# A bidirectional WKV network on one core: products, means and gelu of neighbouring steps put in another order

## The chip, the cores and the metric

The kernel runs on one core of a Trainium2 chip. The metric is the time of the program on the device in microseconds (us), the median of several runs. The engines are PE (TensorE: matmuls), DVE (VectorE), ACT (ScalarE), POOL (GpSimd) and SP, which here only issues DMAs. Each engine works through its own instructions in the order in which the program issues them, and semaphores make it wait for the others.

## The reference

x has shape (16, 192, 56, 56). Three layers of one kind are followed by a fourth of another, and each adds its result to x:

```python
x = x + _L0_conv_ref(_gn(x), ...)   # and L1, L2: the same with other weights
x = x + _L3_conv_ref(_gn(x), conv_w, ...)
```

`_gn` normalises groups of 6 channels over the image. One of the first three layers computes, for the T = 3136 positions of an image:

```python
k, v, r = xs @ Wk.T, xs @ Wv.T, xs @ Wr.T
x_fwd = wkv_scan(real_w, u, k, v)                    # a decaying sum along T, numerator over denominator
x_bwd = flip(wkv_scan(real_w, u, flip(k), flip(v)))  # the same from the end
h = sigmoid(r) * 0.5 * (x_fwd + x_bwd)
h = layernorm(h)                                     # over channels
out = h @ Wo.T
```

The fourth layer takes the largest difference to the four pixels two rows or columns away, puts it beside x, multiplies 384 channels by a 192 x 384 matrix, and applies a normalisation with constants and gelu.

## The kernel before, in words

**Tiling.** Images are taken in eight pairs. With 192 channels a pair has 384, which lie in three column blocks j of 128 partitions; a tile is 128 x 3 x 448 floats, and a pair has NL = 7 such chunks (L = 448 positions). A `Run` is one pair in one layer.

**Two passes.** A WKV layer goes over the chunks forwards (units "A") and then backwards (units "B"). Unit A forms k (`a_keys`), exp k (`a_exp`), v (`a_values`), their product (`a_ekv`, L940), the two scans on DVE (`a_q`, `a_p`, L875), denominator and numerator with the bonus (`a_den`, `a_num`, L890), inverts the denominator by ln and exp on ACT (`invert`, L975 and L978) and multiplies on POOL (`a_y`, L982). Unit B scans backwards (`b_q`, `b_p`), adds the bonus (`b_den`, `b_num`), inverts, forms r on PE (`b_gate`: `product`, L597 to L607) and the sigmoid of r on ACT in two halves (`b_exp`, L996, an exp that reads r; `b_sigmoid`, L1003 and L978), and mixes on POOL (`b_mix`, nine operations, L1031 to L1033). Then comes layernorm: squares on ACT (`b_squares`, L1040), sums over channels on PE (`b_sums`, L1047 and L1049), the square of the mean on ACT (`b_rs1`, L1055), its subtraction by a matmul (`b_rs2`, L1059), ln and exp on ACT (`b_rs3`, L1063 and L1065), the spread over partitions on PE (`b_spread`, L1071), the scaling on DVE (`b_scale`, L1076), the output product (`b_out`), the addition to x (`b_x`, L1089, called by `add`), and the new chunk's statistics on ACT (`b_stats`, by `sum_up`).

**The conv layer** has units "C": `c_rows` and `c_columns` on DVE (L1108 to L1129), two products accumulated in the same PSUM banks (`c_product` with half 0 and 1), `c_gelu` on ACT (L1150, with a table load before it and one after it, L1155), `c_add` on POOL (L1159) and the store by SP.

**Order.** Two streams of pairs are interleaved: while one run goes backwards, a run of the other goes forwards. The list `steps` holds 249 steps (numbered from 0 here), each with a B unit, a front unit (A or C), or one of them. `with tc.manual_schedule(...)` has each engine's instructions in the order in which the step functions issue them, so the order is written out by hand:

- `both_a_first` (L1379) and `both_a` (L1323): a B and an A unit. There are 17 groups of one first step and five `both_a`, which begin at steps 8, 16, 24, 32, 40, 78, 86, 94, 102, 140, 148, 156, 164, 202, 210, 218 and 226. In the nine groups of 24, 32, 40, 86, 94, 102, 148, 156 and 164, the five `both_a` steps also compute statistics of a pair still to come (`count`, `z_stats`, L734 and L735); the other eight hold none or next to none.
- `both_c` (L1426): a B and a C unit; seven groups of six, at 48, 63, 110, 125, 172, 187 and 234. In all but the last group, the fifth step starts the next pair (`begin_later`) and the sixth has the first A unit of that pair behind it (`ahead`).
- `forward_a`, `forward_c`, `backward_alone` (L1667) and `neither`: steps with one unit or none.

What is late is carried over: a B unit's layernorm begins in its own step and ends in the next (`late[u]` holds its stage). `nback` and `nfront` are the next step's units. In `both_a` the next unit's r is formed at the head of a step (`b_gate(*nback[1:])`, L1330), read by `b_exp` at once, and the layernorm's sums stand last on PE in the step (L1367).

The normalisation ahead of a layer is folded into its weights in four parts (`norm_sums`, `norm_var`, `norm_fold`, `norm_fold_r`), which `gap()` takes one at a time from the list `norms` wherever a step calls it. When conv products are still outstanding (`convs`), the next run is put into `waiting` and its weights are loaded behind the last of these products (`conv_part`). `store()` writes out the chunk that `c_add` has put into `stores` before.

Of the kernel before, what the change touches and what calls it, by code (L numbers as in the profile page):

```python
# [55 lines left out]
NL = T // L  # L56
# [417 lines left out]
def fast_path(ctx: ExitStack, tc: tile.TileContext, flag, x, wproj, wfold, wcfold, wconst, wgroup, sums, picks, vecs, out):  # L474
# [345 lines left out]
        load_ahead(("C" if run.l == NLAYERS else "A", run, 0))  # L820

    def gap(eng=V):
        if norms:
            part, run = norms.pop(0)
            if part is norm_fold:
                part(run, eng)
            else:
                part(run)
# [155 lines left out]


    def b_gate(run, c):
        product(run, "r", run.w[2], run.xb[c], c == NL - 1)

    def b_exp(run, c):
        if c == NL - 1:  # L990
# [166 lines left out]
    def c_add(run, c):  # L1157
        xs, g = run.xa.pop(c), run.ml.pop(c)
        G.tensor_add(g.t, g.t, xs.t)  # L1159
        xs.give()  # L1160
        if c == NL - 1:
            require_all(run.chk, slice(3 * NL + 9, NCHK))
        stores.append((run, c, g))

    def c_end(run, c, more):
# [154 lines left out]
        for _ in range(min(most, len(z))):  # L1320
            z_stats(*z.pop(0))

    def both_a(b, a, nback, nfront, z, loads):  # L1323

        den = lambda: a[0].den[a[1]]
        l = of_stage(0.5)
        load_ahead(nback)
        store()
        if nback is not None:
            b_gate(*nback[1:])  # L1330
            b_exp(*nback[1:])
        count(z)
        b_q(*b)
        if l:
            b_rs2(*l)
            b_rs3(*l)
        b_sigmoid(*b)
        a_values(*a)
        if l:
            b_spread(*l)  # L1340
        b_p(*b)
        b_den(*b)
        for js in (AC, slice(1, 2)):
# [12 lines left out]
        keys(nfront)  # L1356
        a_q(*a)
        if l:
            add(l)
        b_squares(*b, (0,))  # L1360
        a_save(*a)
        count(z)
        exp_keys(nfront, (0, 2))
        b_squares(*b, (2,))
        exp_keys(nfront, (1,))
        b_squares(*b, (1,))
        b_sums(*b)  # L1367
        a_p(*a)
        gap()
        a_den(*a)  # L1370
        b_rs1(*b)
        late[b] = 0.5
        invert(den())
        gap()
        a_num(*a)
        a_y(*a)
        gap()

    def both_a_first(b, a, nback, nfront, loads):  # L1379

        den = lambda: a[0].den[a[1]]
        l = of_stage(0)
        load_ahead(nback)
        store()
        a_values(*a)
        b_squares(*l, (0, 2))
        b_q(*b)
        b_sigmoid(*b)
        b_p(*b)
        b_den(*b)  # L1390
        invert(b[0].ek[b[1]])
        b_num(*b)
        b_mix(*b)
        for u in loads:
            load_ahead(u)
        a_ekv(*a)
        b_squares(*l, (1,))
        if nback is not None:
            b_gate(*nback[1:])
        b_sums(*l)  # L1400
        b_rs1(*l)
        if nback is not None:
            b_exp(*nback[1:])
        a_q(*a)
        b_rs2(*l)
        b_rs3(*l)
        keys(nfront)
        a_p(*a)
        spread_and_scale(l)
        b_squares(*b, (0,))  # L1410
        a_save(*a)
        exp_keys(nfront)
        b_squares(*b, (2, 1))
        b_sums(*b)
        a_den(*a)
        b_rs1(*b)
        late[b] = 0.5
        invert(den())
        a_num(*a)
        add(l)  # L1420
        a_y(*a)
# [4 lines left out]
    def both_c(b, a, nback, nfront, loads):  # L1426

        l0, l1 = of_stage(0), of_stage(1.5)
        load_ahead(nback)
        first = nback is not None and not l1  # L1430
        store()
        b_q(*b)
        b_p(*b)
        if l1:
            b_out(*l1)
        if first:

            b_gate(*nback[1:])
            b_exp(*nback[1:])
            c_product(*a, 0)  # L1440
        if half:
            c_product(*half[0], 1)
        if l0:
            b_squares(*l0, (0,))
        sum_up()
        if l0:
            b_squares(*l0, (2, 1))
            b_sums(*l0)
        if l1:
            add(l1)  # L1450
        b_den(*b)
        invert(b[0].ek[b[1]])
        if l0:
            b_rs1(*l0)
            b_rs2(*l0)
            b_rs3(*l0)
        gap()
        if half:
            u = half.pop()
            c_gelu(*u, False)  # L1460
            c_add(*u)
        for u in loads:
            load_ahead(u)
        if nback is None:
            keys(nfront)
            exp_keys(nfront)
        elif not first:
            b_gate(*nback[1:])
            b_exp(*nback[1:])
        if l0:  # L1470
            b_spread(*l0)
        if not first:
            c_product(*a, 0)
        c_rows(*a)
        gap()
        c_columns(*a)
        gap()
        b_num(*b)
        b_sigmoid(*b)
        b_mix(*b)  # L1480
        if nback is not None:
            if l0:
                b_scale(*l0)
                late[l0] = 1.5
            b_q(*nback[1:])
            b_p(*nback[1:])
            half.append(a)
        else:
            ahead = nfront is not None and nfront[0] == "A"
            if ahead:  # L1490
                a_q(*nfront[1:])
                a_save(*nfront[1:])
            c_product(*a, 1)
            c_end(*a, False)
            if ahead:
                a_values(*nfront[1:])
            if l0:
                b_scale(*l0)
                b_out(*l0)
                late[l0] = 2  # L1500
        late[b] = 0
# [165 lines left out]
    def backward_alone(b, nback, nfront):  # L1667
        load_ahead(nback)
        load_ahead(nfront)
        store()  # L1670
        sum_up()
        b_q(*b)
        gap()
        b_den(*b)
        gap()
        invert(b[0].ek[b[1]])
        b_sigmoid(*b)
        b_p(*b)
        gap(G)
        b_num(*b)  # L1680
        b_mix(*b)
        for u in list(late):
            finish(u)
        if nback is not None:
            b_gate(*nback[1:])
            b_exp(*nback[1:])
        keys(nfront)
        exp_keys(nfront)
        late[b] = 0
# [13 lines left out]
    with tc.manual_schedule(engines={PE.engine, V.engine, S.engine, G.engine, nc.sync.engine}):  # L1703
# [6 lines left out]
        for i, (b, f, z) in enumerate(steps):  # L1710
            nback, nfront, _ = steps[i + 1] if i + 1 < len(steps) else (None, None, None)
            for run in starts.get(i, ()):
                begin_later(run)
            if i == 0:
                keys(f)
                exp_keys(f)
            ahead = [("Z", run, c) for run, c, _ in (z if not b else [])]
            ahead += [nfront] if b and f else []
            ahead += [("Z", run, c) for run, c, _ in (steps[i + 1][2] if i + 1 < len(steps) else [])]
            ahead += [steps[i + 2][0]] if i + 2 < len(steps) else []  # L1720

            nkeys = nfront if nfront is not None and nfront[0] == "A" else None
            if f and not b and nkeys is None and nfront is not None and i + 2 < len(steps):
                far = steps[i + 2]
                if far[0] is None and far[1] is not None and far[1][0] == "A" and far[1][1] is f[1]:
                    nkeys = far[1]
            if f and nback is None and nfront is not None:
                near = [u for _, u, _ in steps[i + 1 : i + 4] if u is not None and u[0] == "A"]
                if len(near) > 1 and near[1][1] is near[0][1]:
                    ahead.append(near[1])  # L1730
            if not (b and f):
                for u in ahead:
                    load_ahead(u)
            if b and f and f[0] == "A":
                if of_stage(0) is None:
                    both_a(b[1:], f[1:], nback, nfront, z, ahead)
                else:
                    both_a_first(b[1:], f[1:], nback, nfront, ahead)
            elif b and f:
                both_c(b[1:], f[1:], nback, nfront, ahead)  # L1740
            elif f and f[0] == "A":
                forward_a(f[1:], nback, nfront, nkeys, z)
            elif f:
                forward_c(f[1:], nback, nfront)
            elif b:
                backward_alone(b[1:], nback, nfront)
            else:
                neither(nback, nfront)
            assert not z
# [102 lines left out]
```

## Time and profile before

| | |
|---|---|
| median of 3 runs | 5206.31 us (5205.58 to 5208.39) |
| the profiled execution | 5220.16 us |
| its span in the trace | 5218.2 us |
| mean granted PE clock | 0.935 of full |
| PE / DVE / ACT / POOL busy | 4733.3 / 4750.5 / 3684.6 / 2889.2 us |
| instructions | 51856 |
| HBM traffic | 324.83 MB read, 154.14 MB written, 92 GB/s |

The profile is one execution, recorded by the hardware. Its page gives totals and the costliest groups of instructions; windows give busy time by stage, and the timeline gives each instruction's start and length and, in brackets, how long its engine had stood idle and what released it. Lines as L1049 are lines of the kernel. The profiled execution is 13.85 us longer than the median, so durations are weighed against its own 5220.16 us.

### The profile page before, as it was taken

To read this page: it belongs to the slowest core of one execution; us is meant where nothing else is said; L and a number is where in the kernel's file an instruction comes from. 1 tells how busy PE (TensorE), PEld (TensorE's weight loads), DVE (VectorE), ACT (ScalarE), POOL (GpSimd) and SP (SyncE) were. 2 spreads that over 40 slices of the span, in tenths; PEclk is the share of its full clock that TensorE was granted. 3 is DMA by queue.
4 is the path that set the end of the run, shared out by engine and by line. 5 is a ranking of instruction groups with operands and counts; after the bars stand their busy time and mean duration, and the time that the engine had idled before them with its cause. 6 is when DMAs were issued, how large, how long until landed. Compare 5 with 4: busy or idle time off the path is not lost. (4 is left out here: it accounts for less than half of the span.)

```text
span 5218.2 us, 51856 instructions
## 1 busy us (share of the span) xinstructions
PE 4733.3 (91%) x15542; PEld 1498.8 (29%) x15542; DVE 4750.5 (91%) x6271; ACT 3684.6 (71%) x7163; POOL 2889.2 (55%) x2251
## 2 busy tenths in 40 slices
PE   7899998989899999998989999999898999999897
PEld 3222222223232222222323222222232322222222
DVE  6999999998989999999898999999889899999995
ACT  6777787776566777787656678777756667777772
POOL 1665665554545656565454556556545455666562
PEclk8999999999899999999989999999998999999998
DMA  5222222233232222223233223222333322222233
GB/s 154 69 82 87 90 86 89 85 110 97 90 116 72 87 90 93 82 90 122 93 93 101 84 75 100 88 85 87 128 93 101 93 74 77 72 84 77 80 104 120
DMA packets 314274, 482.47 MB, mean 92 GB/s; under 512 B 66432, under 2 KB 306688, under 8 KB 313984
## 3 DMA queue, kind: packets, MB, share of 16 engines
q1 hardware_dynamic: 312832, 477.59, 28.5%
q8 instruction: 126, 2.06, 0.2%
q10 hardware_dynamic: 1152, 1.48, 0.1%
q14 instruction: 164, 1.34, 0.1%
HBM read 324.83 MB, written 154.14 MB: 92 GB/s over the span
## 5 line engine op out<-in xcount | busy, mean ns | idle before, releaser
L875 DVE TENSOR_TENSOR_SCAN q<-fdecays,ek 128x449 f32<-128x449 f32 (+1 forms) x1008 | 1023.4, 1068 | 28.0 <-ACT ek L920 25.4
L875 DVE TENSOR_TENSOR_SCAN p<-fdecays,ekv 128x449 f32<-128x449 f32 (+1 forms) x1008 | 1020.3, 1065 | 0.6
L982 POOL TENSOR_TENSOR p<-p,q 128x1344 f32<-128x1344 f32 x168 | 512.0, 3047 | 830.3 <-ACT q L978 546.9
L1031 POOL TENSOR_TENSOR ekv<-ekv,ek 128x448 f32<-128x448 f32 x504 | 602.7, 1196 | 456.1 <-ACT ek L978 385.3
L1033 POOL TENSOR_TENSOR p<-p,sg 128x448 f32<-128x448 f32 x504 | 638.0, 1266 | 57.2 <-ACT ek L884 12.7
L1032 POOL TENSOR_TENSOR p<-p,ekv 128x448 f32<-128x448 f32 x504 | 606.1, 1203 | 39.5
L1040 ACT ACTIVATE ek<-p 128x448 f32<-128x448 f32 x504 | 286.4, 572 | 309.4 <-POOL p L1033 308.9
L886 POOL COPY ekv<-p 128x3 f32<-128x3 f32 x282 | 233.1, 827 | 488.0 <-DVE p L875 457.2
L1076 DVE TENSOR_TENSOR p<-p,rsb 128x448 f32<-128x448 f32 x504 | 282.4, 613 | 194.5 <-PE rsb L1071 194.4
L920 ACT ACTIVATE ek<-k,k 128x448 f32<-128x448 f32 x504 | 297.2, 632 | 225.3 <-PE k L601 179.2
L735 ACT ACTIVATE fjunk<-x 128x448 f32<-128x448 f32 x672 | 387.7, 577 | 40.1 <-DVE x L1089 13.4
L1071 PE MATMUL rsb<-rs,fpicks 32*128 32x448 f32 (+1 forms) x1008 | 359.2, 629 | 42.4 <-ACT rs L1065 42.4
L1159 POOL TENSOR_TENSOR ml<-ml,x 128x1344 f32<-128x1344 f32 x56 | 178.9, 3194 | 391.8 <-ACT ml L1150 391.8
L890 DVE SCALAR_TENSOR_TENSOR ek<-ek,fcc,q 128x896 f32<-128x896 f32 x336 | 379.1, 1167 | 0.0
L890 DVE SCALAR_TENSOR_TENSOR q<-ek,fcc,q 128x896 f32<-128x896 f32 x336 | 359.2, 1109 | 6.3 <-ACT cvb L954 4.6
L1089 DVE SCALAR_TENSOR_TENSOR x<-ops,fwob,x 128x448 f32<-128x448 f32 x504 | 314.2, 670 | 46.7 <-PE ops L601 26.6
L734 ACT ACTIVATE fjunk<-x 128x448 f32<-128x448 f32 x600 | 342.5, 571 | 11.4
L996 ACT ACTIVATE sg<-r,r 128x448 f32<-128x448 f32 x504 | 313.0, 627 | 33.5 <-PE r L607 20.7
L890 DVE SCALAR_TENSOR_TENSOR ekv<-ekv,fcc,p 128x896 f32<-128x896 f32 x336 | 330.1, 1022 | 0.0
L940 DVE SCALAR_TENSOR_TENSOR ekv<-v,v,ek 128x448 f32<-128x448 f32 x504 | 312.5, 672 | 16.6 <-PE v L601 8.0
L975 ACT ACTIVATE q<-q 128x1344 f32<-128x1344 f32 x168 | 221.5, 1318 | 125.5 <-DVE q L890 101.3
L890 DVE SCALAR_TENSOR_TENSOR p<-ekv,fcc,p 128x896 f32<-128x896 f32 x336 | 295.3, 919 | 6.5 <-POOL ekv L886 1.7
(235 smaller groups left out, 11546.4 us busy)
## 6 DMA issues: line engine op xcount, KB each, us to landing
x<-xd SPq DMA_DIRECT2D x240, 672.0 KB, 5.3
xd<-x SPq DMA_DIRECT2D x168, 672.0 KB, 3.9
x<-in_x_dram SPq DMA_DIRECT2D x320, 224.0 KB, 4.3
x<-in_x_dram SPq DMA_DIRECT2D x320, 112.0 KB, 4.2
out_dram<-ml SPq DMA_DIRECT2D x112, 224.0 KB, 2.3
m<-xd SPq DMA_DIRECT2D x112, 168.0 KB, 5.1
wkv<-in_wfold_dram SPq DMA_DIRECT2D x24, 640.0 KB, 5.6
out_dram<-ml SPq DMA_DIRECT2D x112, 112.0 KB, 2.3
```

What stands on the lines that cost most here:

```text
L734: S.activation(junk, xt[:, j, :], AF.Identity, accum_out=stats[:, 0, j, c : c + 1])
L735: S.activation(junk, xt[:, j, :], AF.Square, accum_out=stats[:, 1, j, c : c + 1])
L875: V.tensor_tensor_scan(out, dec[:, column(j)].to_broadcast([P, L if first else L + 1]), e, 0.0, ALU.mult, ALU.add)
L890: by_channel(lambda js, i: V.scalar_tensor_tensor(dst.t[:, js, :], e.t[:, js, :], cc[:, i : i + 1], state.t[:, js, :], ALU.mult, ALU.add))
L940: V.scalar_tensor_tensor(e.t[:, j, :], ps[j][:, 0:L], b[:, j, :], run.ek[c].t[:, j, :], ALU.add, ALU.mult)
L982: G.tensor_mul(run.h[c].t, run.h[c].t, den.t)
L996: S.activation(sg.t[:, j, :], ps[j][:, 0:L], AF.Exp, bias=b[:, j, :], scale=-1.0, accum_out=run.chk[:, at : at + 1])
L1031: G.tensor_mul(y.t[:, j, :], y.t[:, j, :], den.t[:, j, :])
L1032: G.tensor_add(h.t[:, j, :], h.t[:, j, :], y.t[:, j, :])
L1033: G.tensor_mul(h.t[:, j, :], h.t[:, j, :], sg.t[:, j, :])
L1071: PE.matmul(ps[j][:, :L], pick[rows, j, :], rs[rows, :], start=True, stop=True)
L1089: V.scalar_tensor_tensor(xj, ps[j][:, 0:L], wob[:, column(j)], xj, ALU.add, ALU.add, accum_out=run.new[:, 0, j, c : c + 1] if c == 0 else ...
```

## The change

- `gap` doesn't take `norm_fold` of a run that is in `waiting`.
- `b_gate` forms a unit's r only once. `both_a` and `both_a_first` get `far`, the B unit two steps ahead if it is of the same run, and form its r just ahead of `b_sums` of their own unit. So the next step's `b_gate(nback)` finds it done.
- `c_add` issues the earlier chunk's `store()` before it registers its own.
- `both_a_first`: `a_q` and `a_ekv` go ahead of `b_den`; rs2 and rs3 follow rs1 directly, ahead of `b_exp`; `a_save` moves ahead of `a_p`; the spread, the scaling and the output product move ahead of `keys`.
- `both_c`: a `gap()` moves to the head, ahead of `b_out`; `add(l1)` moves ahead of the later squares; `invert` is split, and rs1 and rs2 are issued between its ln and its exp, rs3 behind; `c_add` moves from behind gelu to behind `b_mix`. In the last step of a group that has an A unit behind it, both products of the chunk go into `convs`, where the products of the last chunk already went, and are formed in the later `forward_a` steps, two chunks instead of one; `a_values` follows `a_save`.
- `backward_alone`: `gap(G)` (there `norm_fold`) moves ahead of the sigmoid.

The diff, without the renaming of a variable in the main loop (`far` to `then`) and the passing on of `far` in the calls:

```diff
--- before.py
+++ after.py
@@ -820,7 +820,7 @@
         load_ahead(("C" if run.l == NLAYERS else "A", run, 0))
 
     def gap(eng=V):
-        if norms:
+        if norms and not (norms[0][0] is norm_fold and norms[0][1] in waiting):
             part, run = norms.pop(0)
             if part is norm_fold:
                 part(run, eng)
@@ -984,7 +984,8 @@
 
 
     def b_gate(run, c):
-        product(run, "r", run.w[2], run.xb[c], c == NL - 1)
+        if once(run, "r", c):
+            product(run, "r", run.w[2], run.xb[c], c == NL - 1)
 
     def b_exp(run, c):
         if c == NL - 1:
@@ -1160,6 +1161,7 @@
         xs.give()
         if c == NL - 1:
             require_all(run.chk, slice(3 * NL + 9, NCHK))
+        store()
         stores.append((run, c, g))
 
     def c_end(run, c, more):
@@ -1320,7 +1322,7 @@
         for _ in range(min(most, len(z))):
             z_stats(*z.pop(0))
 
-    def both_a(b, a, nback, nfront, z, loads):
+    def both_a(b, a, nback, nfront, z, loads, far):
 
         den = lambda: a[0].den[a[1]]
         l = of_stage(0.5)
@@ -1364,6 +1366,8 @@
         b_squares(*b, (2,))
         exp_keys(nfront, (1,))
         b_squares(*b, (1,))
+        if far:
+            b_gate(*far[1:])
         b_sums(*b)
         a_p(*a)
         gap()
@@ -1376,7 +1380,7 @@
         a_y(*a)
         gap()
 
-    def both_a_first(b, a, nback, nfront, loads):
+    def both_a_first(b, a, nback, nfront, loads, far):
 
         den = lambda: a[0].den[a[1]]
         l = of_stage(0)
@@ -1387,30 +1391,32 @@
         b_q(*b)
         b_sigmoid(*b)
         b_p(*b)
+        a_q(*a)
+        a_ekv(*a)
+        b_squares(*l, (1,))
         b_den(*b)
         invert(b[0].ek[b[1]])
         b_num(*b)
         b_mix(*b)
         for u in loads:
             load_ahead(u)
-        a_ekv(*a)
-        b_squares(*l, (1,))
         if nback is not None:
             b_gate(*nback[1:])
         b_sums(*l)
         b_rs1(*l)
+        b_rs2(*l)
+        b_rs3(*l)
         if nback is not None:
             b_exp(*nback[1:])
-        a_q(*a)
-        b_rs2(*l)
-        b_rs3(*l)
-        keys(nfront)
+        a_save(*a)
         a_p(*a)
         spread_and_scale(l)
+        keys(nfront)
         b_squares(*b, (0,))
-        a_save(*a)
         exp_keys(nfront)
         b_squares(*b, (2, 1))
+        if far:
+            b_gate(*far[1:])
         b_sums(*b)
         a_den(*a)
         b_rs1(*b)
@@ -1431,6 +1437,7 @@
         store()
         b_q(*b)
         b_p(*b)
+        gap()
         if l1:
             b_out(*l1)
         if first:
@@ -1443,22 +1450,22 @@
         if l0:
             b_squares(*l0, (0,))
         sum_up()
+        if l1:
+            add(l1)
         if l0:
             b_squares(*l0, (2, 1))
             b_sums(*l0)
-        if l1:
-            add(l1)
         b_den(*b)
-        invert(b[0].ek[b[1]])
+        ln(b[0].ek[b[1]])
         if l0:
             b_rs1(*l0)
             b_rs2(*l0)
+        exp_minus(b[0].ek[b[1]])
+        if l0:
             b_rs3(*l0)
-        gap()
-        if half:
-            u = half.pop()
-            c_gelu(*u, False)
-            c_add(*u)
+        ended = half.pop() if half else None
+        if ended:
+            c_gelu(*ended, False)
         for u in loads:
             load_ahead(u)
         if nback is None:
@@ -1469,7 +1476,8 @@
             b_exp(*nback[1:])
         if l0:
             b_spread(*l0)
-        if not first:
+        ahead = l0 and nback is None and nfront is not None and nfront[0] == "A"
+        if not first and not ahead:
             c_product(*a, 0)
         c_rows(*a)
         gap()
@@ -1478,6 +1486,8 @@
         b_num(*b)
         b_sigmoid(*b)
         b_mix(*b)
+        if ended:
+            c_add(*ended)
         if nback is not None:
             if l0:
                 b_scale(*l0)
@@ -1485,15 +1495,17 @@
             b_q(*nback[1:])
             b_p(*nback[1:])
             half.append(a)
+        elif ahead:
+            a_q(*nfront[1:])
+            a_save(*nfront[1:])
+            a_values(*nfront[1:])
+            b_scale(*l0)
+            b_out(*l0)
+            late[l0] = 2
+            convs.extend(((a, 0), (a, 1)))
         else:
-            ahead = nfront is not None and nfront[0] == "A"
-            if ahead:
-                a_q(*nfront[1:])
-                a_save(*nfront[1:])
             c_product(*a, 1)
             c_end(*a, False)
-            if ahead:
-                a_values(*nfront[1:])
             if l0:
                 b_scale(*l0)
                 b_out(*l0)
@@ -1674,9 +1686,9 @@
         b_den(*b)
         gap()
         invert(b[0].ek[b[1]])
+        gap(G)
         b_sigmoid(*b)
         b_p(*b)
-        gap(G)
         b_num(*b)
         b_mix(*b)
         for u in list(late):
@@ -1731,11 +1743,14 @@
             if not (b and f):
                 for u in ahead:
                     load_ahead(u)
+            far = steps[i + 2][0] if nback is not None and i + 2 < len(steps) else None
+            if far is not None and far[1] is not nback[1]:
+                far = None
```

More of the change, by code (lines that the diff above doesn't have):

```diff
@@ L1723, in fast_path @@
             if f and not b and nkeys is None and nfront is not None and i + 2 < len(steps):
-                far = steps[i + 2]
-                if far[0] is None and far[1] is not None and far[1][0] == "A" and far[1][1] is f[1]:
-                    nkeys = far[1]
+                then = steps[i + 2]
+                if then[0] is None and then[1] is not None and then[1][0] == "A" and then[1][1] is f[1]:
+                    nkeys = then[1]
             if f and nback is None and nfront is not None:
@@ L1733, in fast_path @@
                     load_ahead(u)
+            far = steps[i + 2][0] if nback is not None and i + 2 < len(steps) else None
+            if far is not None and far[1] is not nback[1]:
+                far = None
             if b and f and f[0] == "A":
                 if of_stage(0) is None:
[L1736 removed]
+                    both_a(b[1:], f[1:], nback, nfront, z, ahead, far)
                 else:
[L1738 removed]
+                    both_a_first(b[1:], f[1:], nback, nfront, ahead, far)
             elif b and f:
```

## The prediction, made before the changed kernel had run

> **What bounds the kernel now.** First the busy totals, which only say that two engines are nearly full on average; then the windows by stage; then the timeline inside one step of each kind. The page's part 1:
>
> ```profile
> PE 4733.3 (91%) x15542; PEld 1498.8 (29%) x15542; DVE 4750.5 (91%) x6271; ACT 3684.6 (71%) x7163; POOL 2889.2 (55%) x2251
> ```
>
> Windows, one step each: a both_a step without statistics (450), one with them (570), a both_c step (1138.6). The columns are length, then busy us and instruction count of each engine, granted clock, DMA share, GB/s.
>
> ```profile
> 258.00:281.00 23.00, 22.08 (x78) 6.35 (x76) 23.00 (x29) 18.73 (x37) 15.30 (x12) 1.00 0.15 50
> 570.00:597.20 27.20, 25.11 (x83) 7.77 (x82) 25.27 (x31) 21.66 (x46) 16.85 (x14) 0.94 0.31 102
> 1138.60:1163.10 24.50, 22.72 (x81) 7.07 (x80) 21.46 (x31) 18.85 (x35) 15.08 (x12) 1.00 0.38 127
> ```
>
> (The first row lies in step 11; I read steps 18 and 19, of the same kind.) Three stages, three limits. Plain both_a steps: DVE 23.00 of 23.00, so DVE bounds; a step is 23.57 long (step 18's first DVE instruction at 388.90, step 19's at 412.48). Counted steps: 27.1, with DVE at 25.27 and a clock of 0.94, so a ring of waits bounds. both_c: 24.47, no engine full, so again a ring.
>
> The ring of a counted step, from step 26's timeline (start, us, engine, line; the wait and its releaser in brackets):
>
> ```profile
> 592.60 2.59 DVE L890 SCALAR_TENSOR_TENSOR q<-ek,fcc,q 128x896 f32<-128x896 f32 x2
> 592.67 2.04 POOL L1033 TENSOR_TENSOR p<-p,sg 128x448 f32<-128x448 f32 x1
> ...
> 594.74 0.58 ACT L1040 ACTIVATE ek<-p 128x448 f32<-128x448 f32 x1 [2.53 <-POOL p L1033]
> 594.76 0.14 PEld L1049 LDWEIGHTS st<-p,fsums 128*32 128x32 f32 x4 [2.89 <-POOL p L1033]
> 594.76 1.50 PE L1049 MATMUL st<-p,fsums 128*32 128x448 f32 x4 [2.08 <-POOL p L1033]
> ...
> 597.12 0.54 ACT L1055 ACTIVATE rs<-st 64x448 f32<-64x448 f32 x1 [1.81 <-PE st L1049]
> ```
>
> b_mix's last product on POOL releases the last square, then the sums, and only then PE comes to r; r releases b_exp, which delays the sigmoid, the inverse of ek and the next b_mix. The wait for r is in the same step's ACT rows:
>
> ```profile
> 575.20 0.63 ACT L996 ACTIVATE sg<-r,r 128x448 f32<-128x448 f32 x1 [0.53 <-PE r L607]
> ```
>
> In the plain step POOL and DVE miss each other by 0.09 us (b_mix's last product ends at 409.09, a_den starts at 409.18) and both run short:
>
> ```profile
> 407.94 1.15 POOL L1033 TENSOR_TENSOR p<-p,sg 128x448 f32<-128x448 f32 x1
> ...
> 409.18 1.72 DVE L890 SCALAR_TENSOR_TENSOR q<-ek,fcc,q 128x896 f32<-128x896 f32 x2
> ```
>
> In both_c, ACT (step 50):
>
> ```profile
> 1147.57 0.52 ACT L1055 ACTIVATE rs<-st 64x448 f32<-64x448 f32 x1
> 1149.15 0.63 ACT L1063 ACTIVATE rs<-st,feps 64x448 f32<-64x448 f32 x1 [1.05 <-PE st L1059]
> 1149.81 0.57 ACT L1065 ACTIVATE rs<-rs 64x448 f32<-64x448 f32 x1
> 1150.40 1.28 ACT L1150 ACT_TABLE_LOAD   x1
> 1151.70 1.96 ACT L1150 ACTIVATE ml<-cv,cvb,finv 128x448 f32<-128x448 f32 x3
> ```
>
> ACT stands 1.05 us for PE's rs2 each step, with the table load, gelu, b_exp and the sigmoid behind it.
>
> **The change, part by part.** Seventeen groups of six steps (one both_a_first, five both_a) hold the first two edits; eight groups count nothing, nine do.
>
> *r ahead, plain groups.* The r product (7 matmuls, 4.58 us) leaves the head of a step for the place before b_sums one step earlier. The instructions are the same. PE per plain step: r, v, k and the output product 4 x 4.58, rs2 0.96, spread 1.97, sums 1.64: 22.9, less 0.07 of overlap at each of seven joints, 22.4. New waits: rs2 now stands directly behind the sums and waits for rs1 (step 16 shows that join: 0.65), and spread waits for rs3: rs3 ends some 6.6 after the sums (0.05 + rs1 0.54 + inverse 2.64 + b_exp 1.87 + 0.25 + rs3 1.23), spread comes at 6.2 (0.65 + 0.96 + v 4.58), so 0.4. Sum 23.45, under DVE's 23.57. b_exp waited 0.17 for r here, so there is nothing to win: DVE sets the end before and after. What can move is only DVE's own durations. In the first step r for the step after next is put ahead of its last sums, so these end 4.3 later (363.56 to about 367.95); r's 4.58 no longer stands between them and rs2, so rs2, v and spread end near 376.0 instead of 375.36, and b_scale starts about 1.05 later than its 374.45. If b_mix then slides over a_den, that costs 2.59 - 1.72 = 0.87 a step. I take the 1.05 and one collision: +1.9, +15 for eight groups. The fourth both_a issues no r; PE idles there, and if the clock halves for one product (step 26's r at half clock: 5.08 against 4.58; a whole one at half clock, step 21's output product: 7.46) DVE waits for at most about 1. Ends: -1 (one POOL copy, 1.03, out of DVE's way) to +5.6 (1.05, four collisions, 1.1), so -8 to +45.
>
> *r ahead, counted groups.* r leaves the ring. Gained: the 0.53 wait and the rest of b_exp's stretch (2.50 against 1.87), say 1.2 a step in three steps; the idle before the sums (2.08) is partly filled by r. Against: the first step's lag of 1.05 and one more 0.5 for rs2's new wait. -3.6 + 1.55 = -2.0, times nine: -18. Ends: -1.7 a step, where r also stays at full clock (0.5 more), -5, to +1 (next late is the 25.27 of DVE plus its wait for the spread, and nothing shrinks): -45 to +9.
>
> A rule that speaks against half of this: the Trainium skill, "TensorE: Matmul & The Clock Gate", Part 1, holds that the PE's clock halves after about 3.4 us of idleness. By it the 2.08 here would not touch the clock, and the 0.5 would be no gain; but the row after those 2.08 us is an r of 5.08 at a granted clock of 0.94, so I keep 0.5 as an end only. "GPSIMD Engine Reference", 1. Specifications, says that GpSimd shares its SBUF interfaces with VectorE operations of two SBUF inputs; the 2.59 and 2.04 above agree. By it alone any slide of b_mix costs, which is the first rival.
>
> *First step reordered.* a_q and a_ekv go ahead of b_den, out of whose way the preceding b_mix then is: b_den 3.13 and b_num 3.51 shrink toward 1.72 and 1.74; DVE's idle 3.41 before b_scale shrinks as the spread comes earlier. DVE gains up to 6 us, but PE's order ends the step, and PE gains only what r took: the lag above is already what is left of both. Priced at nothing beyond it.
>
> *both_c: rs1 between ln and exp.* rs2 (0.96) runs beside exp_minus (1.33), so the 1.05 goes; three steady steps a group: -3.15. Next late is DVE: 21.46 busy of 23.4. c_add (3.04) behind b_mix frees POOL earlier, but b_mix's third product waited for the sigmoid already (0.54 at 1159.64): nothing. Its new place lies over c_rows and c_columns, which it stretches (step 52 shows 8.17 against 5.28); the 2.96 of idle DVE a step covers that, and if the cover is gone it costs 2.9. The third step's c_columns writes the buffer whose store now waits for the later c_add: +1.25 (ends 0 and 4).
>
> *backward_alone: fold before the sigmoid.* norm_fold's ACT part stood behind both passes of the sigmoid (2.64), and the first k or conv product waits for it: -2.65 a conv group (ends 0 and -5).
>
> *gap at the head, chunk 5's products late.* Six groups. psg's matmuls now stand ahead of b_out and wait for DVE behind b_p: +3.5 on PE against DVE's 4.77 wait for psg removed: +1.8 (ends 0, +3.7). Two products (9.1) leave step 53 for later steps, so the sums of the next step come up to 8.6 earlier; but chunk 6's products move back in turn, and the next conv weights, queued on SP with the loads of two edge strips and a chunk (4.3 and 5.1 to land), are issued behind them. Both are about 9; at nothing, ends -1.5 and +2.
>
> Conv sum: -3.15 + 1.25 - 2.65 + 1.8 = -2.75 in six groups, -4.5 in the last (no 1.8): -21, say -22 with the ends -45 to +8.
>
> **Sum.** 15 - 18 - 22 = -25 on the profiled execution, which took 5220.16 (span 5218.2 and 1.96 around it): 5195. The median shown is 13.85 below that execution, so the forecast is 5181.
>
> **Rivals.**
> 1. *b_mix slides over DVE in plain groups, slower.* For: POOL clears a_den by only 0.09 us, DVE has no idle, and the lag of 1.05 exceeds 0.09, so it decides as soon as the lag is not worked off in one step. Against: b_mix starts when ACT's inverse of ek and b_num are done, and b_num is DVE's, which the lag does not touch. Price +5 x 8 = +40; with the counted groups at 0 and conv at -12: +28, 5234.
> 2. *The rings give their whole ends.* Counted -45, conv -40, plain 0: 5121. For: 2.08 of idle and a clock of 0.94. Against: DVE is at 25.27 of 27.2.
> 3. *Nothing moves.* r ahead hides a wait (0.17, 0.53) that other waits replace, chunk 5 is only shifted: 5206. For: the small waits; against: 1.05 in 21 steps is plain to see.
>
> **How the numbers follow.** About 0.2% (10 us) is what a measurement of this kernel can tell from no change. Forecast 0.40, rival 1 0.37, rival 2 0.10, rival 3 0.13: faster 0.50, same 0.13, slower 0.37. Both signs hold much. The forecast's own range is 5160 to 5195. The ends of all parts together give -98 and +62; not all fall together: I take 5131 (half of rival 2 in) to 5255 (above rival 1's 5234 by half of the plain groups' spread).
>
> **What would show it.** Plain step: still 23.57, with a_den at 1.72; at 2.59, rival 1. Counted step: 27.1 to about 26, no wait before L996. First step: rs1 of its last sums 4.3 later relative to its first v. both_c: 24.47 to 23.4, no wait before L1063. Step 53 shorter by 9 and steps 57 to 60 longer. I am wrong if a DMA landing sets the steps behind 53, or if the steps without r bring half clock into DVE's waits.

## The result, and the profile after

The changed kernel takes 5492.71 us (median of 4, 5490.66 to 5493.76) against 5205.94 before: 1.0552 times as long, interval 1.0534 to 1.0571, 287 us more. Forecast were 5181 and a range up to 5255. The profiled execution took 5492.79 us, its span is 5491.0.

The page's part 1 after: DVE and PE are longer busy with the same number of instructions (15542 and 6271), so instructions have become slower, and the share of each engine fell, so waits were added too.

```profile
PE 4829.1 (88%) x15542; PEld 1524.7 (28%) x15542; DVE 4885.3 (89%) x6271; ACT 3668.6 (67%) x7163; POOL 2848.8 (52%) x2251
```

The windows of one step each, after, in the columns of before: a plain both_a step (step 19), a counted one (step 28) and a both_c step (step 51).

```profile
434.18:461.50 27.32, 24.61 (x83) 7.59 (x84) 27.32 (x31) 19.03 (x37) 15.19 (x12) 0.94 0.24 76
659.71:687.89 28.18, 22.59 (x86) 6.36 (x82) 27.03 (x31) 21.38 (x45) 15.58 (x12) 0.98 0.38 122
1223.80:1246.95 23.15, 16.98 (x60) 4.72 (x58) 23.08 (x31) 18.74 (x35) 15.47 (x12) 0.99 0.64 204
```

The plain step has gone from 23.57 to 27.3, with DVE still busy throughout. The both_c step of the window went as forecast (23.15, forecast 23.4); the one before it in the group (step 50) went from 24.48 to 29.25. Laying the two traces side by side, step by step at the end of DVE's work, the 272 us of the two spans divide so:

| steps | difference, us |
|---|---|
| 8 plain groups: first step / second / third / fourth and fifth / sixth | +7 / +62 / +6 / +57 / -3 = +128 |
| 9 counted groups: first / second / the other four | +10 / +79 / +3 = +91 |
| 6 conv groups with the forward steps behind them | +51 |
| the last conv group and all else | +2 |

The +51 is rather too small: the execution traced before took some 14 us more than its median, and runs below that change nothing in the conv groups are there 7 to 28 us shorter than it.

The waits of the changed kernel name what is late (us in total, times, longest):

```profile
POOL p L982 <- ACT q L978: 780.7, 113, 20.7
POOL ekv L1032 <- ACT ek L978: 428.6, 97, 5.8
ACT ek L920 <- PE k L601: 415.3, 107, 11.1
POOL ekv L1032 <- DVE ekv L890: 350.5, 33, 22.2
```

Before, the first of these (a_y on POOL waiting for the inverse) was 546.9, and the third (exp of k waiting for k) 179.2. The timeline of steps 18 and 19 shows the first at work (the columns are start, length, engine, line; brackets give the idle time and its releaser). Before, a_y began 1.52 us into step 19, whose window starts at 412.48, and was over when b_den began:

```profile
414.00 3.06 POOL L982 TENSOR_TENSOR p<-p,q 128x1344 f32<-128x1344 f32 x1 [3.65 <-ACT q L978]
418.39 1.72 DVE L890 SCALAR_TENSOR_TENSOR ek<-ek,fcc,q 128x896 f32<-128x896 f32 x2
```

After, it begins 5.88 us into the step, whose window starts at 434.18:

```profile
436.82 0.54 ACT L1056 ACTIVATE rs<-st 64x448 f32<-64x448 f32 x1 [5.07 <-PE st L1050]
437.26 1.31 ACT L975 ACTIVATE q<-q 128x1344 f32<-128x1344 f32 x1
438.60 1.33 ACT L978 ACTIVATE q<-q 128x1344 f32<-128x1344 f32 x1
440.06 3.04 POOL L982 TENSOR_TENSOR p<-p,q 128x1344 f32<-128x1344 f32 x1 [8.01 <-ACT q L978]
440.10 4.55 DVE L890 SCALAR_TENSOR_TENSOR ek<-ek,fcc,q 128x896 f32<-128x896 f32 x2
...
457.29 2.62 DVE L890 SCALAR_TENSOR_TENSOR q<-ek,fcc,q 128x896 f32<-128x896 f32 x2
```

rs1 (L1056) waits 5.07 us for the sums, which now stand behind r on PE. The inverse of the denominator stands behind rs1 in ACT's order and runs at once afterwards, so it had only been held up. a_y follows it, lands on the next step's b_den, and b_den takes 4.55 instead of 1.72. That is 2.83 of the step's 3.75 us; a_den, on which b_mix has slid, is the 0.90 that remain (2.62 against 1.72).

### The profile page after: what moved, and what is told of

It reads as the page before. It is cut to its first block, busy times and chain, and to the rows that moved or that the text cites. A ratio compares the mean times of both kernels' runs of the same rounds, so it can differ in the third digit from the quotient of the medians.

```text
span 5491.0 us, 51993 instructions
## 1 busy us (share of the span) xinstructions
PE 4829.1 (88%) x15542; PEld 1524.7 (28%) x15542; DVE 4885.3 (89%) x6271; ACT 3668.6 (67%) x7163; POOL 2848.8 (52%) x2251
## 3 DMA queue, kind: packets, MB, share of 16 engines
q1 hardware_dynamic: 312832, 477.59, 27.1%
## 5 line engine op out<-in xcount | busy, mean ns | idle before, releaser
L1034 POOL TENSOR_TENSOR p<-p,sg 128x448 f32<-128x448 f32 x504 | 617.3, 1225 | 67.9 <-ACT ek L884 20.8
L1072 PE MATMUL rsb<-rs,fpicks 32*128 32x448 f32 (+1 forms) x1008 | 388.8, 666 | 131.8 <-ACT rs L1066 131.8
L890 DVE SCALAR_TENSOR_TENSOR q<-ek,fcc,q 128x896 f32<-128x896 f32 x336 | 427.8, 1314 | 39.8 <-ACT ek L884 35.1
L890 DVE SCALAR_TENSOR_TENSOR ek<-ek,fcc,q 128x896 f32<-128x896 f32 x336 | 430.4, 1322 | 0.0
L886 POOL COPY ekv<-p 128x3 f32<-128x3 f32 x282 | 197.8, 702 | 326.0 <-DVE p L875 262.1
L890 DVE SCALAR_TENSOR_TENSOR p<-ekv,fcc,p 128x896 f32<-128x896 f32 x336 | 310.8, 967 | 48.3 <-POOL ekv L886 44.8
L598 PE MATMUL ops<-p,fwo 128*128 128x448 f32 x336 | 238.1, 801 | 125.7 <-DVE p L1077 125.6
L975 ACT ACTIVATE ek<-ek 128x896 f32<-128x896 f32 (+1 forms) x253 | 237.1, 937 | 105.2 <-DVE ek L890 105.2
```

The costliest lines, as they stand in the source:

```text
L890: by_channel(lambda js, i: V.scalar_tensor_tensor(dst.t[:, js, :], e.t[:, js, :], cc[:, i : i + 1], state.t[:, js, :], ALU.mult, ALU.add))
L975: S.activation(s.t[:, js, :], s.t[:, js, :], AF.Ln)
L1034: G.tensor_mul(h.t[:, j, :], h.t[:, j, :], sg.t[:, j, :])
L1072: PE.matmul(ps[j][:, :L], pick[rows, j, :], rs[rows, :], start=True, stop=True)
```

## The experiments

Ratios are to the kernel before on the same chip, whose medians were 5201 to 5220. First the parts of the change one by one, then tests of why each part costs what it does.

**r ahead alone.** Only the hunks for `b_gate` and `far`.

> Before, with r ahead of the sums alone (both_a and both_a_first; the first step's order is otherwise that of before). Theory (ACT's order): r's 4.58 us now lie between the squares and the sums, so rs1 comes later; behind rs1 in ACT's order stands the inverse of the denominator, so a_y on POOL comes some 5 us later and falls on the next step's b_den on DVE (1.72 becomes 4.3 to 4.5). Third to fifth step of a plain group 27.0 to 27.3 instead of 23.57, about +7 to +10 a plain group, counted steps about as before: 5270 to 5320. Rival (first step): the loss of the two kinds of groups, 219 us in the profiles, comes from the reordered first step, and r ahead alone stays within 20 us of 5206.

Measured 5317.15, ratio 1.0222 (1.0202 to 1.0242), against 5205.0. The traces: plain groups +88, of it 49 in the fourth and fifth steps, counted groups +31. Half of what the groups lost; the other half is not r's.

**r ahead, and the inverse ahead of rs1.** The same, and in `both_a`:

```diff
-        b_rs1(*b)
-        late[b] = 0.5
         invert(den())
+        b_rs1(*b)
+        late[b] = 0.5
```

> r ahead of the sums as in the run with r ahead alone, and in both_a the inverse of the denominator goes ahead of rs1 in ACT's order. Theory (ACT's order): the inverse no longer waits for the late sums, a_y falls where it fell before, b_den is 1.72 to 1.8 again, plain steps are back near 23.6 to 24.5 and counted ones at 25.5 to 27: 60 us or more below the run with r ahead alone, 5180 to 5230. Rival (PE): the steps are longer because PE waits for rs1, rs3 and b_scale and runs at half clock after that; then this run stays within 20 us of the run with r ahead alone.

Measured 5192.64, ratio 0.9973 (0.9962 to 0.9983): 125 us come back by one swapped pair on ACT. Its timeline at the same place:

```profile
420.46 1.33 ACT L975 ACTIVATE q<-q 128x1344 f32<-128x1344 f32 x1 [1.81 <-DVE q L890]
421.82 1.33 ACT L978 ACTIVATE q<-q 128x1344 f32<-128x1344 f32 x1
423.28 3.04 POOL L982 TENSOR_TENSOR p<-p,q 128x1344 f32<-128x1344 f32 x1 [3.46 <-ACT q L978]
423.72 0.54 ACT L1056 ACTIVATE rs<-st 64x448 f32<-64x448 f32 x1 [0.58 <-PE st L1050]
427.85 1.73 DVE L890 SCALAR_TENSOR_TENSOR ek<-ek,fcc,q 128x896 f32<-128x896 f32 x2
```

a_y is over 1.5 us before b_den starts, which is 1.73 again, though r still stands ahead of the sums. So the ACT order is the cause in the third to fifth steps, and PE's own new waits are not. (Not all of the 125 us is what rs1 had held up: some 25 to 33 us of it the swap brings without r ahead, as the next run shows.) In the counted groups the third to fifth steps are 1.4 to 3.1 us shorter than before. The second step of each group still loses 4.0, in this run as in the one before. The swap was made in `both_a` only: in the first step rs1 still stands ahead of the inverse, and r, put ahead of that step's last sums, makes it wait. The start of the second step in this run:

```profile
373.19 0.54 ACT L1056 ACTIVATE rs<-st 64x448 f32<-64x448 f32 x1 [10.15 <-PE st L1050]
375.74 4.54 DVE L890 SCALAR_TENSOR_TENSOR ekv<-ekv,fcc,p 128x896 f32<-128x896 f32 x2
376.44 3.37 POOL L982 TENSOR_TENSOR p<-p,q 128x1344 f32<-128x1344 f32 x1 [13.74 <-ACT q L978]
```

Before, this rs1 waited 5.27, a_y began 3.74 us into the step instead of 8.25, and b_num took 1.73. So 2.8 of the 4.0 is the same cause at a place that the swap didn't reach; in the counted groups 2.1 to 2.8, on b_num or b_den. No run has the inverse ahead of rs1 in `both_a_first`, so this part is read from the trace and not tested.

**The inverse ahead of rs1 alone.** The swap without r ahead.

> Before, with the inverse of the denominator ahead of rs1 in both_a alone, r where it was. Theory: r still stands behind the sums on PE and b_exp waits for it, so the earlier inverse wins nothing by itself: 5195 to 5215. Rival: the gain of 125 us between the two runs with r ahead is the inverse's own, whatever r does: 5150 or below.

Measured 5186.94, ratio 0.9952 (0.9937 to 0.9966). I had expected nothing and was wrong: the swap is worth half a per cent by itself. The traces put about 16 us of it in the forward steps behind groups: they are 15 to 17 us shorter in every run with the swap and at most 5 in those without. Another 17 are in conv steps, but runs that change nothing there differ from the trace of before by as much, so these can't be given to the swap. Why the forward steps gain isn't settled. The rival's 5150 was not reached either, and with r where it was the third to fifth counted steps kept their length to within 1.6 us.

**The first step reordered alone.** Only the hunk of `both_a_first`, without `far`.

> Before, with the reordered both_a_first alone (r stays where it was). Theory: b_den and with it the inverse, b_mix and rs1 of the step come later (in the changed kernel b_mix of this step starts at 361.1 minus 345.7 = 15.4 us after the step's first scan instead of 14.5, and k stands behind the output product), which the next step's b_scale waits for; about 7.3 us a group were seen in the second step with r ahead, 4.6 of them r's own: +3 a group, 17 groups, 5255. Rival: the order is harmless by itself, DVE's shorter b_den and b_num pay for it: 5190 to 5210.

Measured 5327.25, ratio 1.0234 (1.0217 to 1.0251): the direction was expected, but less than half of the size. The trace of its step 16 shows DVE holding itself up, a_q waiting for exp k ahead of b_den, and a_num later for a copy on POOL behind b_mix:

```profile
345.63 3.05 DVE L875 TENSOR_TENSOR_SCAN q<-fdecays,ek 128x448 f32<-128x448 f32 x3 [2.44 <-ACT ek L920]
351.27 1.74 DVE L890 SCALAR_TENSOR_TENSOR ek<-ek,fcc,q 128x896 f32<-128x896 f32 x2
...
367.69 1.75 DVE L890 SCALAR_TENSOR_TENSOR p<-ekv,fcc,p 128x896 f32<-128x896 f32 x2 [3.58 <-POOL ekv L886]
```

b_den itself is short now, 1.74 instead of 3.13, but it comes 14.1 us after the step's first scan instead of 5.9.

**The reorder with DVE's part put back.**

```diff
         b_p(*b)
-        a_q(*a)
-        a_ekv(*a)
-        b_squares(*l, (1,))
         b_den(*b)
...
+        a_ekv(*a)
+        b_squares(*l, (1,))
         if nback is not None:
             b_gate(*nback[1:])
...
             b_exp(*nback[1:])
+        a_q(*a)
         a_save(*a)
```

> The reordered first step alone, but with a_q and a_ekv left behind b_den as before (rs2 and rs3 behind rs1, b_exp, a_save and keys as in the reorder). Theory: the whole reorder cost 122 us because a_q and a_ekv, which wait for k's exp and for v, now hold b_den up on DVE, so b_mix starts 4 us later in the step and a_y falls on the next b_den (4.50 against 1.72); with b_den back in its place this goes: 5195 to 5225. Rival: rs3 ahead of b_exp and k behind the output product cost as much: 5270 or above.

Measured 5290.33, ratio 1.0175 (1.0158 to 1.0192): the rival. DVE's part is worth a quarter; the larger cause is on PE. The timeline of step 16, before:

```profile
350.05 0.96 PE L1059 MATMUL st<-rs,fpicks 64*64 64x448 f32 x2 [0.65 <-ACT rs L1055]
350.94 1.02 PE L598 MATMUL k<-x,wkv 128*128 128x448 f32 x2
...
355.45 1.97 PE L1071 MATMUL rsb<-rs,fpicks 32*128 32x448 f32 x6
```

And in this run:

```profile
354.57 0.96 PE L1059 MATMUL st<-rs,fpicks 64*64 64x448 f32 x2 [0.66 <-ACT rs L1055]
...
356.86 3.41 PE L1071 MATMUL rsb<-rs,fpicks 32*128 32x448 f32 x6 [1.32 <-ACT rs L1065]
...
360.20 1.86 PE L598 MATMUL ops<-p,fwo 128*128 128x448 f32 x2
```

Before, k stood between rs2 and the spread and covered rs3. Without it PE waits 1.32 right after 0.66, and then its clock falls (0.50 granted from 357.3 to 364.1, 0.65 on average over the spread and the output product, 1.00 before): the spread takes 3.41 against 1.97, the output product 6.45 against 4.58. 1.32 of waiting, 1.44 and 1.87 in these two and 1.25 in the sums behind (a wait of 0.32 in it) are 5.9 us, and the second step is 5.1 to 6.7 longer.

**With k back between rs2 and the spread.**

```diff
         a_p(*a)
-        spread_and_scale(l)
         keys(nfront)
+        spread_and_scale(l)
```

> The run with the rest of the reordered first step (1.75% slower than before), with one thing put back: k stands between rs2 and the spread on PE again. Theory: without k there, PE waited 0.66 for rs1 and 1.32 for rs3 within 2.3 us, its clock halved (the spread took 3.41 instead of 1.97, the output product 6.45 instead of 4.58), the sums ended 6 us later, and DVE waited 8.34 for the next step's spread; with k in its place all of this goes: 5195 to 5215, 75 us or more below that run. Rival: rs3 ahead of b_exp, or the earlier a_save, costs it: 5270 or above.

Measured 5203.94, ratio 0.9969 (0.9957 to 0.9980): all of it is gone. So k's place costs all of it, 86 us between the two runs, and rs3 ahead of b_exp costs nothing.

**The conv order alone**: rs1 and rs2 between ln and exp, `add` earlier, `c_add` behind `b_mix`, its `store()`.

> Before, with the changes inside both_c that leave the two late products and the gaps out: rs1 between ln and exp, add ahead of the later squares, c_add behind b_mix, the earlier store in c_add. Theory: the third step of each group loses 4.8 to 6 because c_columns waits for the store of its buffer, whose c_add is now behind b_mix; the fourth and fifth gain about 1.2 each, the second up to 3: +2 a group, 5206 + 14 = 5220. Rival: the store's wait is worked off by the shorter steps behind it: 5185 to 5200.

Measured 5189.32, ratio 0.9972 (0.9957 to 0.9987), in the rival's range. The third step of a group does lose 4.6 to 6.1, but the fifth wins 5.5 to 6.1 in six of the seven groups, which I had not seen.

**rs1 between ln and exp alone** (with the earlier `add`; `c_add` stays behind gelu).

> rs1 and rs2 between the inverse's ln and exp in both_c, and add ahead of the later squares, alone: the run with the conv order (5189) without c_add behind b_mix. Theory: the 1.05 us on ACT goes in some four steps of seven groups, 20 to 30 us in all, and c_columns of the third step does not wait for a store: 5175 to 5190. Rival: the gain of the conv order was c_add's (c_columns no longer beside it): then 5200 or above here.

Measured 5163.29, ratio 0.9921 (0.9904 to 0.9937). ACT in step 50 of this run:

```profile
1143.57 1.33 ACT L975 ACTIVATE ek<-ek 128x1344 f32<-128x1344 f32 x1
1145.37 0.54 ACT L1055 ACTIVATE rs<-st 64x448 f32<-64x448 f32 x1 [0.48 <-PE st L1049]
1145.81 1.31 ACT L978 ACTIVATE ek<-ek 128x1344 f32<-128x1344 f32 x1
1147.15 0.63 ACT L1063 ACTIVATE rs<-st,feps 64x448 f32<-64x448 f32 x1
```

The wait ahead of L1063, 1.05 before, is gone. This is the best part of the change; moving `c_add` gives back half a per cent of it.

**The conv order with the gap at the head.**

```diff
         b_p(*b)
+        gap()
         if l1:
             b_out(*l1)
```

(and the `gap()` behind the inverse removed.)

> The run with the conv order (5189) with the gap at the head of both_c added. Theory: in a group's fifth step the normalisation's matmuls stand ahead of the output product on PE and wait for DVE's reduction, which stands behind both backward scans; b_x on DVE then waits over 7 us for the output product; without the gap this step had won 5.8 a group: +8 to +9.5 in six groups, 5235 to 5250. Rival (as predicted): DVE's wait for these matmuls goes in exchange, +1.8 a group at most: 5189 to 5200.

Measured 5243.73, ratio 1.0057 (1.0036 to 1.0077), so the gap costs 0.85%. The same step in the changed kernel (step 52):

```profile
1246.86 0.17 DVE L740 TENSOR_REDUCE mv<-zstats 128x6 f32<-128x42 f32 x1
1247.18 0.56 PE L612 MATMUL psg<-mv,fgmat 128*128 128x2 f32 x2 [5.02 <-DVE mv L740]
...
1254.15 1.28 DVE L1090 SCALAR_TENSOR_TENSOR x<-ops,fwob,x 128x448 f32<-128x448 f32 x2 [7.12 <-PE ops L601]
```

PE stands 5.02 for a reduction of 0.17 us that is queued behind two scans, and DVE then stands 7.12 for the product queued behind that on PE.

**The late products alone.**

> Before, with the late products alone: both products of the conv chunk in a group's last step go to the later forward steps (and norm_fold waits for its weights). Theory (SP's queue): the next conv weights' load waits on SP for PE's last late product and the chunk that the last k needs is queued behind it; that k waits some 6 us for it, DVE 6 to 11 us in two steps a group, against 5 to 8 won in the step after the last: +4 to +7 in six groups, 5230 to 5250. Rival: the two ends cancel, as predicted: 5198 to 5214.

Measured 5240.04, ratio 1.0045 (1.0030 to 1.0059). The step behind the group wins 6.1, two later ones lose 0.8 to 6.9 and 5.6 to 11.9. In the changed kernel (step 60), SP's queue and the waiting k:

```profile
1387.45 0.33 SPq L813 DMA_DIRECT2D wkv<-in_wcfold_dram  x1
...
1389.18 0.55 SPq L547 DMA_DIRECT2D x<-in_x_dram  x1
...
1393.61 1.83 PE L598 MATMUL k<-x,wkv 128*128 128x448 f32 x2 [6.19 <-DMA x<-in_x_dram]
```

The weights' DMA had stood at the head of SP's queue for 48.4 us, waiting for PE's last late product. It is issued behind the second of four late products (`half == 1` is true for each chunk), while the last one still reads its buffer.

**The same, with the weights behind the last product.**

```diff
-                while waiting:
+                while waiting and not convs:
```

> The run with the late products (0.45% slower than before), with one condition added: the next weights are loaded behind the last late product and not behind the second of four, where the load's DMA stood at the head of SP's queue for 48 us (its buffer was still read by PE) with the chunk for the last k behind it. Theory: the wait of 6 us for that chunk goes and the 6 us won in the step behind the group remain: 20 to 45 us faster than the run with the late products, 0.1 to 0.5% below before. Rival: the load is now too late for norm_fold, whose run starts two steps on: no faster than that run.

Measured 5198.05, ratio 0.9992 (0.9982 to 1.0001): the mended condition saves 0.5%, and the cause is shown. What is left is no gain that can be measured.

**Putting the good parts together.** r ahead and the inverse first, r only in counted groups (`if not any(len(s[2]) > 1 for s in steps[i : i + 2]): far = None`), the conv order, the earlier fold.

> r ahead of the sums and the inverse ahead of rs1, r ahead in the counted groups alone, with the conv order (without the gap at the head and without the late products) and the earlier fold in backward_alone. Sum of the parts: the counted groups won 27 with r ahead and the inverse first, the plain ones lost 45 in that run, the conv order won 16, the fold some 8 (2.8 in every other group): 5205 - 27 - 16 - 8 = 5154. Theory: the parts lie in different steps and add: 5140 to 5170. Rival: the two streams' waits take the place of each other and less than half is left: above 5180.

Measured 5123.01, ratio 0.9826 (0.9791 to 0.9861): the parts add, and more. The earlier fold was run alone nowhere; in the trace of the changed kernel the first conv step is 2.2 to 2.8 shorter in four of the seven groups and as long as before in three.

**With another buffer for c_columns** (`Slot("ml", V)`).

> The candidate (1.7% faster than before) with the buffer of c_columns taken from those that DVE used last, so that the third step of a conv group does not wait for the store of a chunk that c_add has only just added. Theory: the 5 us a group in the third step (4.8 to 6.0) go, 7 groups: 25 to 38 us below the candidate, 5085 to 5100. Rival: the following steps had made the wait good, or the scans of b_q and b_p now wait for stored buffers instead: within 10 us of the candidate.

Measured 5111.41, ratio 0.9824 (0.9808 to 0.9841): the rival. The wait of 3.4 in the third step is gone in all seven groups, and these steps are together 25 us shorter in the traces; the ratios show no gain. With the interval of the run before it at 0.35% either way, whether the time is gone too stays open.

**With c_add back behind gelu.**

> The candidate (1.7% faster than before) with c_add back behind gelu; rs1 between ln and exp in both_c stays. Theory: rs1 inside the inverse alone gave 0.8% and with c_add moved 0.3%, so c_add's move costs 0.5% here too: about 2.2% faster than before, 5085 to 5105. Rival: with the other streams' steps shortened the conv steps' gain is limited by something else: within 8 us of the candidate.

Measured 5091.2, ratio 0.9759 (0.9742 to 0.9775), as the theory had it.

**With r ahead begun in the second step** (the two lines of `far` in `both_a_first` left out).

> The second candidate, with r ahead not begun in the first step of a group but in the second. Theory: the second step of a counted group loses 3.6 us because the first step's sums end 4.6 us later behind an r; begun later, the second step has two r products on PE (29.5 us busy against 27): 1 us a group won in nine groups, about 10 us below the second candidate. Rival: the second product in one step costs its whole 4.58 there: no gain, or 10 us above.

Measured 5052.95, ratio 0.9683 (0.9667 to 0.9699): 165 us below before on that chip, and the best version. The gain was four times what I expected. In the previous run the spread of the second step waited 1.57 for rs3 and the output product behind it took 6.22; here neither is seen.

```profile
551.60 1.97 PE L1072 MATMUL rsb<-rs,fpicks 32*128 32x448 f32 x6 [1.57 <-ACT rs L1066]
571.99 1.97 PE L1072 MATMUL rsb<-rs,fpicks 32*128 32x448 f32 x6
```

a_y also comes earlier, 3.4 us into that step instead of 7.9, clear of b_num, so the gain can't be divided between the two. The window of a counted step (step 27) of this kernel:

```profile
589.47:614.11 24.64, 23.30 (x92) 7.21 (x84) 24.55 (x30) 21.56 (x46) 15.67 (x12) 1.00 0.24 85
```

24.6 us instead of 27.1, at a full clock and with DVE busy almost throughout: the ring of waits has become DVE's own length.

The ratios of the parts multiply to the whole: r ahead 1.0222, first step 1.0234, conv order 0.9972, gap 1.0057 / 0.9972 = 1.0085, late products 1.0045: 1.057, against 1.0552 measured, which is within the intervals of the parts (the earlier fold isn't among them).

## Why the prediction was wrong

*What bounds.* Right as far as it went. Plain steps are DVE's, counted ones a ring, and breaking the ring wins 2.5 us a step once the rest is in order. Wrong was the conclusion that a DVE-bound step can lose only through a_den.

*r ahead, plain groups* (+15 forecast; +88 in the trace of r ahead alone). This is the step that failed. I priced the new waits on PE (0.65 and 0.4; measured 0.66 and 0.31) and asked what waits for the later sums there. I did not ask it for ACT: rs1 waits for the sums, and behind rs1 stood the inverse of the denominator, which needs no sums at all. My sum for rs3 even counted "inverse 2.64" behind rs1. rs1's wait of 5.07 put the inverse and a_y 4.4 us later in the step, from a place over the scans to one over b_den. The collision that I feared (b_mix over a_den, 0.87) did come, at 0.90, but beside one three times as large. Rival 1 had the kind of mechanism right and the wrong pair of instructions.

*r ahead, counted groups* (-18; +31). The ring did open, as the run with the inverse first shows (third to fifth steps 1.4 to 3.1 us shorter). Here too rs1 blocked it, and the second step's loss was put at 1.05 plus 0.5; it is 4.0, of which 2.1 to 2.8 is again a_y on b_num or b_den, as read above. The 0.5 for the clock was kept as an end only, on a misread row: the r behind the 2.08 wait took 5.27, and the clock granted in the 3.3 us after that wait (595.1 to 598.4) was 0.50; 5.08 is the r of one step earlier, 0.94 the mean of a step.

*First step reordered* ("priced at nothing beyond it"; 122 us). The largest miss. I worked out that spread waits for rs3 only in `both_a`, where v lies between rs2 and the spread. In `both_a_first` the reorder takes away k, the product that lay there. The row of before had it: rs2 at 350.05, k to 355.52, spread at 355.45. And the clock belonged in the sum: 1.98 us of waits within 3 us were followed by 3.3 us more in the next two products. Of the 122 us, the run with k back shows 86 to be k's place; the rest went with DVE's order.

*both_c.* rs1 between ln and exp: right, and larger than forecast (38 us by the medians; -3.15 a group were 22). c_add, priced at +1.25 a group or 9 in all, costs 22 between the traces with and without it, 26 by the medians of two chips. *gap*: I set PE's 3.5 against DVE's 4.77 (4.54 to 4.64 in the trace) and took +1.8; DVE's wait did not go, it moved to b_x and grew to 7.12, and the gap costs some 9 a group instead of 1.8. *Fold*: -2.65 was taken in all seven groups; three of them show nothing. *Late products*: "at nothing", with "a DMA landing sets the steps behind 53" named as a way to be wrong. That came true, by a condition in the code that I had read and not followed.

*Chances.* Slower had 0.37. The range ended at 5255 because its ends were worked out from the collisions that I had named; the bounds of a step are no bounds when a queue behind it was left out.

## What to carry to other kernels

When an instruction is made to wait longer, write down for its engine everything queued behind it in program order, and for each whether it needs what is waited for; whatever doesn't belongs in front. A matmul group that stands between a small result and its use is a cover: before moving it, name what will stand there instead, and count a halved clock into the price of a gap. An engine without idle time can still get slower, by what another engine is moved onto.

## What the runs showed of the hardware

A POOL operation can stop a DVE operation for its whole length, and not share with it: a_y ran from 440.06 to 443.10 in its usual 3.04 us, b_den started at 440.10 and ended at 444.65, 1.55 after a_y. In step 50 after, a DVE maximum of 0.50 us took 3.36 beside c_add. The two rows of the changed kernel:

```profile
1201.45 3.67 POOL L1160 TENSOR_TENSOR ml<-ml,x 128x1344 f32<-128x1344 f32 x1
1202.12 3.36 DVE L1116 TENSOR_TENSOR m<-m,x 128x336 f32<-128x336 f32 x1
```

The scans are not touched: with a_y over them (423.28 to 426.32, inverse first) they take 3.06 and 3.04. The Trainium skill, "SBUF — State Buffer", SBUF: two separate sides, holds that the port pair of the two engines is locked for a whole instruction by whichever starts first, against VectorE operations of two SBUF inputs; a_y, 0.04 us ahead of b_den, and c_add, 0.67 ahead of the maximum, agree. "TensorE: Matmul & The Clock Gate", Part 1, puts the clock's fall at some 3.4 us of idleness; here waits of 0.66 and 1.32, close together, were followed by 0.50 over the next 6.8 us, and in the trace of before a single wait of 2.08 by 0.50 over the next 3.3, so the measurement decides.
